# Making some of a layer's products one layer earlier: nine blocks' direct products in a four-layer sparse graph kernel

## The chip, the cores and the metric

The kernel runs on one core of a Trainium2 chip. The metric is the device time of one execution in microseconds (us). Three runs of the kernel before took 962.64, 964.93 and 965.73 us; the median is 964.93.

A core has five engines that work beside each other, each going through its own list of instructions in order: PE (TensorE, the matrix products), DVE (VectorE), ACT (ScalarE), POOL (GpSimd, which here starts the gathers) and SP (SyncE, which here starts plain transfers). Products are added up in PSUM, everything else lies in SBUF.

## The reference: what is computed

`x` has 2708 rows of 512 numbers; `adj` is a 2708 x 2708 matrix, nearly all zeros, whose nonzeros are denser towards low rows and low columns. Four layers follow, each `x = layernorm(x + gnn(x))`. The two that the change touches:

```python
# layer 0
adj_hat = adj + eye
d = 1 / sqrt(adj_hat.sum(axis=1))
gnn = (d[:, None] * adj_hat * d[None, :] @ x) @ W.T + b
# layer 1
head = (adj > 0) / sqrt(number of positive entries in the row)
inc = adj + head                                  # the "incidence"
gnn = (inc @ x) / inc.sum(axis=1)
```

Layer 2 sums rows under attention weights and under `adj` itself, and uses the projection `h = x @ W_sa`; layer 3 uses signs of a weight matrix. All is float32.

## The kernel before: tiles, stages and order

**Blocks.** The rows are cut into 22 blocks of 128 (the last, block 21, has 20). Four loops, one for each layer, go over the blocks in one order: `sequence` = 0, 1, 21, 2, 3, ... 20. The place of a block in it is its *turn* (block 1 has turn 1, block 2 turn 3, block 11 turn 12, block 12 turn 13, block 13 turn 14).

**Tiles.** For a block, only the columns of `adj` that hold a nonzero in its rows matter. A preparing stage (to about 199 us) finds them and packs the block's part of `adj` into tiles of 128 columns, `packed[b]`. There are two kinds:
- *direct* tiles: a whole block of columns taken as it lies (column block 0 or 1, the dense ones). `DIRECT` lists them: 20 tiles in 15 blocks. Their rows of `x` already lie in SBUF (`place_of_x(0)`, `place_of_x(1)`), so nothing is fetched.
- *gathered* tiles: 98 in all. The 128 rows of `x` that belong to the packed columns are fetched by an indirect DMA that POOL starts (`gathered`, the transfer at L626) into one of a ring of buffers `xg`. After every few gathers a memset (L636) pauses POOL. Some gathered tiles are *narrow*: they serve only 32 or 64 of the block's 128 rows; two to four of them, for different rows, run beside each other on PE.

Every product of a tile is issued by `add_tile` (L1393). One 128 x 512 float32 product shows as two PE instructions in the profile.

**Layer 0** (about 200 to 353 us). For each block: gathers from `y_rows` (ten buffers), the products, then on DVE the combination with the block's own rows (L1508) and the layernorm, which leaves the new x1 in SBUF, and a write of these rows to `x1_rows` in HBM. Two turns behind, `grow1` (L1445 to L1459) adds the finished block's share to block 0's sum of layer 1, `sum1`: block 0 is so dense that it takes every block of columns as it lies; DVE makes the incidence (L1450, L1453) and PE the product (L1454). Beside that, the table `between` hands small steps to the turns. Those that matter here are the head values of layer 1: the blocks lie in nine groups (`GROUPS`), and group n has its positive entries counted at turn 2 + 2n and the row of its values, `head_row`, kept at turn 3 + 2n (L1239). So the direct tiles of a block can be used for layer 1 only when x1 of blocks 0 and 1 is there, and the incidence only when its group's `head_row` is.

**Layer 1** (about 353 to 569 us). For each block but 0: gathers from `x1_rows` (eight buffers, a pause after every two), the incidence of all its tiles on DVE (two operations for each run of tiles, L1674 and L1675), the products (direct tiles first, then whole gathered ones, then narrow ones, `in_turns`), and `finish1`: ACT makes the own share, `t = own1 * x1` (L1586), DVE adds `rdeg` times the sum in PSUM (L1587), then layernorm and a write to `x2_rows`. Then `project1` makes `h` of an earlier block for layer 2 (four transposes L1612, sixteen products L1619), and `grow2` adds to block 0's sums of layer 2 (L1652, L1653).

**Layers 2 and 3** (to the end) take `x2_rows` and what follows in the same manner (gathers L1820, products L1844, L2099, L2138).

**What sets the order.** The program is traced in the order of its Python; a scheduler then fixes the order of instructions of every engine when the program is built. POOL's gathers are chained to one another and to the pauses in the order in which they are traced. On the chip, each engine follows its list, and waits at an instruction until what it needs is there.

Two lines tell where direct and gathered tiles part:

```python
nd = len(direct(b))
src = {i: place_of_x(direct(b)[i]) for i in range(nd)}
```

Of the kernel before, what the change touches and what calls it, by code (L numbers as in the profile page):

```python
# [8 lines left out]
F32 = mybir.dt.float32  # L9
# [10 lines left out]
P = 128  # L20
# [36 lines left out]
)  # L57


WHOLE3 = 5  # L60
AHEAD3 = 5
FETCHES3 = 3
# [445 lines left out]
def sparse_layers(ctx, tc, x, adj, adj_t, w0_t, b0, w_sa, a_sa, w_gcnb, b_gcnb, wa, ba, wb, bb, w3_t,  # L508
# [26 lines left out]
    def tiles(b: int) -> int:  # L535
        return len(direct(b)) + ROOM[b]
# [815 lines left out]
        t, spans = i - len(direct(b)), SPANS[SPLIT[b]]  # L1352
        return spans[t][1:] if 0 <= t < len(spans) else (0, rows(b))

    def whole_runs(b: int, most: int, apart: bool = False):

        nd, n = len(direct(b)), narrow(b)
        whole = [i for i in range(tiles(b)) if not nd <= i < nd + n]
        runs = []
        for i in whole:  # L1360
            if runs and sum(runs[-1]) == i and runs[-1][1] < most and not (apart and i == nd + n):
                runs[-1] = (runs[-1][0], runs[-1][1] + 1)
            else:
                runs.append((i, 1))
        return runs
# [31 lines left out]
    def last_of(b: int, i: int, order):  # L1397
# [3 lines left out]
            span(b, j)[1] <= r0 or span(b, j)[0] >= r1 for j in order[order.index(i) + 1 :]  # L1401
        )

    sum1 = ps_mm.tile([P, D], F32, tag="sum1", name="l1_0", bufs=1)
    with tc.tile_pool(name="s_l0", bufs=10, reuse_waits="tile") as lp:


# [37 lines left out]
        def grow1(j: int):  # L1445

            r = rows(j)
            inc = lp.tile([P, P], F32, tag="inc0", name=f"inc0_{j}", bufs=2)
            a = packed[0][:r, j, :]
            nc.vector.scalar_tensor_tensor(  # L1450
                inc[:r], a, 0.0, head0_row[0][:r], op0=ALU.is_gt, op1=ALU.mult
            )
            nc.vector.tensor_tensor(inc[:r], inc[:r], a, op=ALU.add)  # L1453
            nc.tensor.matmul(  # L1454
                sum1, inc[:r], place_of_x(j)[:r, :D], start=(not grown1),
                stop=(len(grown1) == NB - 1),
            )
            grown1.append(j)

        between = {  # L1460
            2: [attention_loads], 4: [lambda: attention_columns(0)],
# [21 lines left out]
        for at, b in enumerate(sequence):  # L1483
            m = rows(b)
            old = place_of_x(b)
            nc.vector.tensor_tensor(old[:m, :D], old[:m, :D], b0_row[:m], op=ALU.add)
            if b:
                nd = len(direct(b))
                order_ = in_turns(b)
                src = {}  # L1490
                for i in order_:
                    if i >= nd:
                        src[i] = gathered(lp, D, y_rows, b, i - nd)
                    else:
                        if direct(b)[i] == b:
                            y_direct[b] = lp.tile([P, D], F32, tag="own", name=f"y_own{b}", bufs=1)
                            nc.sync.dma_start(y_direct[b][:m], y_rows[b * P : b * P + m, :])
                        src[i] = y_direct[direct(b)[i]]
                ps = ps_mm.tile([P, D], F32, tag="mm", name=f"l0_{b}")
                for i in order_:  # L1500
                    r0, r1 = span(b, i)
                    add_tile(ps, b, i, packed[b][:, i, r0:r1], src[i][:, :D], order_)
            else:
                ps = sum0
            if at > 1:
                grow1(sequence[at - 2])
            t = work.tile([P, D], F32, tag="t", name=f"t0_{b}")
            nc.vector.scalar_tensor_tensor(  # L1508
                t[:m], ps[:m], dinv[:m, b : b + 1], old[:m, :D], op0=ALU.mult, op1=ALU.add
            )  # L1510
            layernorm(old[:m, :D], t, m, f"0_{b}")
            nc.sync.dma_start(x1_rows[b * P : b * P + m, :], old[:m, :D])
            for step_ in between.get(at, []):
                step_()
        for b in sequence[-2:]:
            grow1(b)
    l0_ps.close()
# [64 lines left out]
    def finish1(b: int, ps):  # L1582
        m = rows(b)
        new, old = pairs.get(b, (f[b], f[b]))
        t = work.tile([P, D], F32, tag="t", name=f"t1_{b}")
        nc.scalar.activation(t[:m], old[:m, :D], AF.Copy, scale=own1[:m, b : b + 1])  # L1586
        nc.vector.scalar_tensor_tensor(  # L1587
            t[:m], ps[:m], rdeg[:m, b : b + 1], t[:m], op0=ALU.mult, op1=ALU.add
        )
        layernorm(new[:m, :D], t, m, f"1_{b}", on_act=True)  # L1590
        nc.sync.dma_start(x2_rows[b * P : b * P + m, :D], new[:m])

    with tc.tile_pool(name="s_l1", bufs=8, reuse_waits="tile") as lp:
# [67 lines left out]
        for at, b in enumerate(sequence):  # L1661
            m = rows(b)
            if b:
                nd = len(direct(b))
                order_ = in_turns(b)
                src = {i: place_of_x(direct(b)[i]) for i in range(nd)}
                for i in order_:
                    if i >= nd:
                        src[i] = gathered(lp, D, x1_rows, b, i - nd)
                ps = ps_mm.tile([P, D], F32, tag="mm", name=f"l1_{b}")  # L1670
                inc_of = {}

                def incidence(iv, a, row):
                    nc.vector.scalar_tensor_tensor(iv, a, 0.0, row, op0=ALU.is_gt, op1=ALU.mult)  # L1674
                    nc.vector.tensor_tensor(iv, iv, a, op=ALU.add)  # L1675

                for i0, n in whole_runs(b, 3):
                    inc = lp.tile([P, 3, P], F32, tag="inc0", name=f"inc{b}_{i0}", bufs=3)
                    iv = inc[:, :n, :m]
                    incidence(  # L1680
                        iv, packed[b][:, i0 : i0 + n, :],
                        head_row[:, None, b * P : b * P + m].to_broadcast([P, n, m]),
                    )
                    for i in range(n):
                        inc_of[i0 + i] = iv[:, i, :]
                inc = lp.tile([P, P], F32, tag="inc1", name=f"incn{b}", bufs=3)
                for i0, r0, w, a in narrow_views(b):
                    n = a.shape[1]
                    at_ = b * P + r0
                    iv = inc[:, r0 : r0 + n * w].rearrange("p (n i) -> p n i", n=n)  # L1690
                    incidence(
                        iv, a,
                        head_row[:, at_ : at_ + n * w].rearrange("p (n i) -> p n i", n=n),
                    )
                    for i in range(n):
                        inc_of[i0 + i] = iv[:, i, :]
                for i in order_:
                    add_tile(ps, b, i, inc_of[i], src[i][:, :D], order_)
            else:
                ps = sum1  # L1700
            if left and left[0][-1] in sequence[: max(at - 2, 0)]:
                grow2(left.pop(0))
            finish1(b, ps)
            if at:
                project1(sequence[at - 1])
            if at == 1:
                open_block(0, wp2, ps_mm, "mm")
                open_sums(0)
# [521 lines left out]
```

## Time and profile before

One execution was profiled. It took 992.0 us in all; the profile spans 990.3 of it, with a mean granted PE clock of 0.946. That is 2.8% more than the median of the unprofiled runs (964.93).

| | busy, us | share of the span |
|---|---|---|
| PE, products | 860.8 | 87% |
| DVE | 654.7 | 66% |
| POOL | 549.4 | 55% |
| ACT | 381.1 | 38% |

| stage | us from the span's start |
|---|---|
| preparing, packing, projecting | 0 to 199 |
| layer 0 | 199 to 353 |
| passage: last x1 rows written, first gather of them issued at 359.12, its product at 363.58 | 353 to 364 |
| layer 1 | 364 to 569 |
| layers 2 and 3 | 569 to 990 |

How to read it: an engine's busy time is what its instructions took, not what they had to take; a share of 87% is a mean over stages, some of which leave PE no idle time and some of which do. What a moved instruction costs depends on what its engine does at the place from which it is taken and at the place to which it goes, and on who waits for it there.

### The profile page before, as it was taken

How to read it: one execution, taken by the hardware profiler on the slowest of the kernel's cores; microseconds unless marked ns; L12 is line 12 of the kernel's file. 1: busy time of each engine (PE TensorE's matmuls, PEld its weight loads, DVE VectorE, ACT ScalarE, POOL GpSimd, SP SyncE). 2: the span in 40 equal slices, each digit the busy share in tenths (PEclk: the TensorE clock that was granted, in tenths of full speed). 3: DMA queues.
4: the chain of work that ended last, by engine and by line, in shares of the span. 5: the costliest groups of instructions: out<-in, count | busy, mean ns of one | idle time of the engine just before them, and what ended most of it. 6: DMA issues, size and time to landing. Idle time of an engine off the chain costs nothing.

```text
span 990.3 us, 12880 instructions
## 1 busy us (share of the span) xinstructions
PE 860.8 (87%) x3659; PEld 452.2 (46%) x3659; DVE 654.7 (66%) x2538; ACT 381.1 (38%) x822; POOL 549.4 (55%) x660
## 2 busy tenths in 40 slices
PE   1898789759979979999999989988999999599992
PEld 0444344212222324555555634543555555378771
DVE  4888888726657766565654446675888776556685
ACT  2665556100000014554544433333444333254653
POOL 2577888687877647776542054553454320066661
PEclk9998998979989989999999998998999999889996
DMA  9999996466777646777653276786777541299985
GB/s 266 339 336 306 301 310 199 142 193 192 237 211 222 207 132 195 223 220 233 183 176 121 97 249 236 257 276 216 249 274 261 174 149 47 85 316 331 308 249 173
DMA packets 93557, 220.06 MB, mean 222 GB/s; under 512 B 13660, under 2 KB 28364, under 8 KB 93476
## 3 DMA queue, kind: packets, MB, share of 16 engines
q0 software_dynamic: 43008, 127.61, 43.5%
q1 hardware_dynamic: 38520, 76.78, 22.6%
q10 hardware_dynamic: 11948, 14.76, 4.7%
q8 instruction: 31, 0.51, 0.2%
q14 instruction: 50, 0.41, 0.1%
HBM read 178.21 MB, written 31.71 MB: 212 GB/s over the span
## 4 chain that ended last, share of the span: by engine, by line
PE 68%; DVE 14%; DMA 7%; issue 5%; ACT 2%; another core or an unknown queue 2%; POOL 1%; SPq 0%; ACTq 0%; DVEq 0%; POOLq 0%
PE l L1393 17%; PE h L1619 8%; PE e L1844 7%; PE a L1844 7%; PE l L2099 4%; PE pg L1892 4%; PE pc L1892 3%; PE y L1127 3%; PE l L2138 2%; PE l L1454 2%; PE e L1652 2%; PE a L1653 2%; PE px L1953 2%; DVE s_mask L895 2%; DMA xg<-x_rows,i 2%
## 5 line engine op out<-in xcount | busy, mean ns | idle before, releaser
L1093 POOL DMA_INDIRECT a<-in_adj_t_dram,row_at x98 | 111.3, 1136 | 58.7 <-DVE deg L838 26.1
L626 POOL DMA_INDIRECT xg<-x_rows,i x98 | 95.8, 978 | 70.7 <-PE l L1393 37.1
L626 POOL DMA_INDIRECT xg<-y_rows,i x98 | 97.7, 997 | 32.6 <-issue 19.0
L1393 PE MATMUL l<-xg,a 128*32 128x512 f32 (+3 forms) x196 | 86.0, 646 | 12.6 <-DMA xg<-y_rows,i 12.6
L1820 POOL DMA_INDIRECT xg<-x_rows,i x60 | 59.1, 986 | 61.8 <-ACT ae L1575 16.3
L1127 PE MATMUL y<-s_w,xt 128*128 128x512 f32 (+1 forms) x176 | 91.3, 667 | 1.7 <-ACT xt L1119 1.7
L626 POOL DMA_INDIRECT xg<-xw_rows,i x70 | 71.3, 1018 | 38.7 <-issue 15.9
L1820 POOL DMA_INDIRECT a<-x_rows,i x38 | 36.9, 970 | 95.1 <-DVE mask L1578 37.1
L1619 PE MATMUL h<-s_wsa,xt 128*128 128x256 f32 (+3 forms) x352 | 81.9, 385 | 0.0
L1619 PEld LDWEIGHTS h<-s_wsa,xt 128*128 128x128 f32 (+1 forms) x352 | 63.9, 186 | 24.8 <-ACT xt L1614 9.2
L830 ACT ACTIVATE unused<-arow 128x1408 uint8<-128x1408 f32 (+3 forms) x44 | 58.3, 1325 | 3.0 <-DMA x_rows<-s_zero 2.0
L663 ACT ACTIVATE rsqs<-mv 128x1 f32<-128x1 f32 (+2 forms) x56 | 11.3, 202 | 120.7 <-DVE mv L692 58.8
L1844 PE MATMUL a<-xg,a 128*32 128x512 f32 (+2 forms) x120 | 51.2, 629 | 4.3 <-DMA xg<-x_rows,i 4.3
L1127 PEld LDWEIGHTS y<-s_w,xt 128*128 128x128 f32 (+1 forms) x176 | 35.6, 213 | 41.9 <-issue 39.6
L2099 PE MATMUL l<-ws,pw 128*128 128x512 f32 (+1 forms) x210 | 50.8, 394 | 1.7 <-issue 1.2
L1844 PE MATMUL e<-xg,ae 128*32 128x512 f32 (+2 forms) x120 | 47.9, 601 | 1.1 <-issue 1.1
L694 POOL TENSOR_TENSOR rs<-mv,s_neg_half 128x1 f32<-128x1 f32 (+1 forms) x22 | 13.0, 592 | 61.4 <-DVE mv L692 52.0
L1892 PE MATMUL pg<-s_wg,pt 128*128 128x256 f32 (+1 forms) x176 | 45.0, 397 | 1.3 <-ACT pt L1880 1.3
L688 DVE BATCH_NORM_STATS2 st<-t 128x6 f32<-128x512 f32 (+1 forms) x66 | 45.3, 687 | 0.3
L916 PE MATMUL find<-s_sides,s_mask 128*128 128x5 bf16 (+1 forms) x462 | 15.7, 166 | 34.1 <-DVE s_mask L912 25.2
L2099 PEld LDWEIGHTS l<-ws,pw 128*128 128x128 f32 (+1 forms) x210 | 39.4, 190 | 11.9 <-issue 2.9
L1393 PEld LDWEIGHTS l<-xg,a 128*32 128x32 f32 (+3 forms) x196 | 19.8, 146 | 54.4 <-issue 38.6
(307 smaller groups left out, 1995.5 us busy)
## 6 DMA issues: line engine op xcount, KB each, us to landing
arow<-in_adj_dram SPq DMA_DIRECT2D x21, 704.0 KB
arow<-in_adj_dram SPq DMA_DIRECT2D x21, 650.0 KB
x_rows<-f SPq DMA_DIRECT2D x40, 256.0 KB
aw<-in_adj_t_dram SPq DMA_DIRECT2D x21, 320.0 KB
y_rows<-yt ACTq DMA_DIRECT2D x20, 256.0 KB
x_rows<-h SPq DMA_DIRECT2D x19, 257.0 KB
f<-in_x_dram SPq DMA_DIRECT2D x19, 256.0 KB
h_own<-x_rows SPq DMA_DIRECT2D x19, 256.0 KB
```

What stands on the lines that cost most here:

```text
L626: nc.gpsimd.indirect_dma_start(out=t, out_offset=None, in_=src[:, :], in_offset=bass.IndirectOffsetOnAxis(ap=index[b][:, i : i + 1], axis=0),)
L688: nc.vector.bn_stats(st[:m], t[:m])
L830: nc.scalar.activation(unused[:m, : ar.shape[1]], ar, AF.Copy, accum_out=row_sums[:m, b, h : h + 1])
L895: nc.vector.tensor_scalar(mask[:m, c0 : c0 + ar.shape[1]], ar, 0.0, None, op0=ALU.not_equal)
L1093: nc.gpsimd.indirect_dma_start(out=packed[b][:, t + len(direct(b)), :], out_offset=None, in_=adj_t, in_offset=bass.IndirectOffsetOnAxis(ap ...
L1127: nc.tensor.matmul(ps[:m], xt[:, k, :m], w0[:, k, :], start=(k == 0), stop=(k == KC - 1))
L1393: nc.tensor.matmul(ps[r0:r1], weights, moving, start=(i == order[0]), stop=last_of(b, i, order))
L1619: nc.tensor.matmul(ps, xt[:, k, :m], w[:, k, :], start=(k == 0), stop=(k == KC - 1))
L1820: nc.gpsimd.indirect_dma_start(out=g, out_offset=None, in_=x2_rows[:, :], in_offset=bass.IndirectOffsetOnAxis(ap=index[b][:, t : t + 1], a ...
L1844: nc.tensor.matmul(ps[r0:r1], weights, moving, start=(i == order[0]), stop=last_of(b, i, order))
L1892: nc.tensor.matmul(ps, pt[:, k, :m], w[:, k, :], start=(k == 0), stop=(k == KC - 1))
L2099: nc.tensor.matmul(whole[b], p[:r, h, b * P : (b + 1) * P], g[:r, :], start=(j == 0 and h == 0), stop=(j == NB - 1 and h == 1),)
```

## The change

Layer 1's direct products of nine blocks are made in layer 0. A new function `begin1(b)`, called at the end of a turn of layer 0's loop, makes for block b: the incidence of its direct tiles (two DVE operations), their products into a PSUM buffer of their own (two buffers in turn, `sum0` and `t`), the own share `f[b] = own1 * x1` on ACT, and `f[b] += rdeg * sum` on DVE. The turn is the later of the block's own turn plus two and 4 + 2n for its group n, and only turns up to `BEGUN_BY` = 14 are taken: turn 4: block 1; 6: blocks 2 and 3; 8: 4 and 5; 10: 7; 11: 8; 12: 9; 14: 11. These are twelve direct tiles (blocks 1, 3 and 5 have two). The other eight (blocks 13, 14, 15, 16, 17, 20) stay where they were.

In layer 1 those nine blocks then start with their first gathered tile; `finish1` leaves out the ACT copy for them, and its DVE operation takes `f[b]` in place of it. The number of gathers and their order on POOL stay as they were.

The diff, with the moved helper `incidence` (now in one place for both layers) cut out at its old place:

```diff
+BEGUN_BY = 14
...
-    def whole_runs(b: int, most: int, apart: bool = False):
+    def whole_runs(b: int, most: int, apart: bool = False, since: int = 0):
...
-        whole = [i for i in range(tiles(b)) if not nd <= i < nd + n]
+        whole = [i for i in range(since, tiles(b)) if not nd <= i < nd + n]
...
+    def incidence(iv, a, row):
+        nc.vector.scalar_tensor_tensor(iv, a, 0.0, row, op0=ALU.is_gt, op1=ALU.mult)
+        nc.vector.tensor_tensor(iv, iv, a, op=ALU.add)
+
     sum1 = ps_mm.tile([P, D], F32, tag="sum1", name="l1_0", bufs=1)
+    begun = set()
...
+        def begin1(b: int):
+
+            m, n = rows(b), len(direct(b))
+            inc = heads.tile([P, 2, P], F32, tag="incd", name=f"incd{b}", bufs=2)
+            iv = inc[:, :n, :m]
+            incidence(
+                iv, packed[b][:, :n, :],
+                head_row[:, None, b * P : b * P + m].to_broadcast([P, n, m]),
+            )
+            pool, tag = ((ps_mm, "sum0"), (ps_t, "t"))[len(begun) % 2]
+            ps = pool.tile([P, D], F32, tag=tag, name=f"l1d_{b}", bufs=1)
+            for i, j in enumerate(direct(b)):
+                nc.tensor.matmul(
+                    ps[:m], iv[:, i, :], place_of_x(j)[:, :D], start=(i == 0), stop=(i == n - 1)
+                )
+            nc.scalar.activation(
+                f[b][:m], place_of_x(b)[:m, :D], AF.Copy, scale=own1[:m, b : b + 1]
+            )
+            nc.vector.scalar_tensor_tensor(
+                f[b][:m], ps[:m], rdeg[:m, b : b + 1], f[b][:m], op0=ALU.mult, op1=ALU.add
+            )
+            begun.add(b)
+
+        to_begin = {}
+        for b in sorted(DIRECT):
+            at = max(sequence.index(b) + 2, 4 + 2 * GROUPS.index(group_of[b]))
+            if at <= BEGUN_BY:
+                to_begin.setdefault(at, []).append(b)
...
             for step_ in between.get(at, []):
                 step_()
+            for c in to_begin.pop(at, []):
+                begin1(c)
...
-        nc.scalar.activation(t[:m], old[:m, :D], AF.Copy, scale=own1[:m, b : b + 1])
+        own = f[b] if b in begun else t
+        if b not in begun:
+            nc.scalar.activation(t[:m], old[:m, :D], AF.Copy, scale=own1[:m, b : b + 1])
         nc.vector.scalar_tensor_tensor(
-            t[:m], ps[:m], rdeg[:m, b : b + 1], t[:m], op0=ALU.mult, op1=ALU.add
+            t[:m], ps[:m], rdeg[:m, b : b + 1], own[:m, :D], op0=ALU.mult, op1=ALU.add
         )
...
-                order_ = in_turns(b)
+                first = nd if b in begun else 0
+                order_ = [i for i in in_turns(b) if i >= first]
...
-                for i0, n in whole_runs(b, 3):
+                for i0, n in whole_runs(b, 3, since=first):
```

More of the change, by code (lines that the diff above doesn't have):

```diff
@@ L1671, in sparse_layers @@
                 inc_of = {}
-                def incidence(iv, a, row):
-                    nc.vector.scalar_tensor_tensor(iv, a, 0.0, row, op0=ALU.is_gt, op1=ALU.mult)
-                    nc.vector.tensor_tensor(iv, iv, a, op=ALU.add)
-                for i0, n in whole_runs(b, 3):
+                for i0, n in whole_runs(b, 3, since=first):
                     inc = lp.tile([P, 3, P], F32, tag="inc0", name=f"inc{b}_{i0}", bufs=3)
```

## The prediction, made before the changed kernel was run

> **What bounds the kernel now.** I read the page's totals first, then its chain of work.
>
> ```profile
> span 990.3 us, 12880 instructions
> PE 860.8 (87%) x3659; PEld 452.2 (46%) x3659; DVE 654.7 (66%) x2538; ACT 381.1 (38%) x822; POOL 549.4 (55%) x660
> PE 68%; DVE 14%; DMA 7%; issue 5%; ACT 2%; another core or an unknown queue 2%; POOL 1%; SPq 0%; ACTq 0%; DVEq 0%; POOLq 0%
> ```
>
> PE carries two thirds of the chain. The change moves PE work from layer 1 (about 353 to 569 us) into layer 0 (about 200 to 353 us), so I need the busy time of both, window by window. Columns: window, length, busy us of PE, PEld, DVE, ACT, POOL, then the granted PE clock.
>
> ```profile
> 222.00:257.00 35.00, 32.70 (x87) 8.97 (x85) 23.47 (x94) 1.59 (x7) 27.54 (x32) 0.93 0.70 204
> 257.00:284.00 27.00, 21.08 (x75) 6.04 (x74) 16.92 (x70) 1.28 (x6) 22.07 (x26) 0.96 0.77 226
> 284.00:331.00 47.00, 42.40 (x146) 12.52 (x144) 31.47 (x150) 3.85 (x14) 36.07 (x43) 0.95 0.76 224
> 331.00:353.00 22.00, 21.53 (x59) 6.98 (x59) 17.60 (x90) 2.08 (x9) 8.66 (x10) 0.92 0.49 154
> 353.00:364.00 11.00, 7.08 (x11) 2.50 (x11) 7.71 (x33) 3.36 (x6) 4.11 (x5) 0.69 0.34 101
> 400.00:464.00 64.00, 64.00 (x265) 36.47 (x264) 35.87 (x147) 34.20 (x58) 47.81 (x61) 1.00 0.74 221
> 464.00:559.00 95.00, 95.00 (x353) 54.44 (x353) 47.70 (x183) 43.93 (x75) 37.39 (x47) 1.00 0.49 150
> ```
>
> From 400 on PE has no idle time. Layer 0 from 222 to 353 leaves PE 13.3 us idle (2.3, 5.9, 4.6, 0.5), 5.1 of it after 284, where the last four moved tiles lie. PE's timeline tells what the idle is and what the tiles cost (start, us, engine, line, operation, idle before).
>
> ```profile
> 277.26 1.10 PE L1393 MATMUL l<-xg,a 128*128 128x512 f32 x2
> 282.79 2.07 PE L1454 MATMUL l<-f,inc 128*128 128x512 f32 x2 [4.43 <-DVE t L1508]
> ...
> 360.03 3.75 PE L1393 MATMUL l<-f_other,inc 128*128 128x512 f32 x4 [2.19 <-DVE mv L690]
> 363.58 1.96 PE L1393 MATMUL l<-xg,inc 128*128 128x512 f32 x4
> ...
> 397.21 1.26 PE L1393 MATMUL l<-xg,incn 128*32 128x512 f32 x8
> ```
>
> The largest hole, 4.43 us, is a block-0 product waiting for VectorE. At 360 block 1's two direct tiles run while its gathers are still in flight. A 128x512 tile is two instructions whose starts lie 0.43 apart: 0.86 us.
>
> Layer 1 also hangs on the gathers that POOL issues:
>
> ```profile
> 393.59 0.95 POOL L626 DMA_INDIRECT xg<-x_rows,i  x1 [0.16 <-issue]
> ...
> 409.33 0.95 POOL L626 DMA_INDIRECT xg<-x_rows,i  x1 [0.30 <-issue]
> ```
>
> The first is block 3's last gather, and its product starts at 397.68 (inside the row at 397.21), 4.1 us later: it ran as soon as it landed. The second is block 5's last. From 386 to 416 POOL runs without a pause of its own, one gather per 1.4 us; only later does it wait for PE to free buffers, as POOL's waits in 385 to 560 show (total, times, longest):
>
> ```profile
> POOL xg L626 <- PE l L1393: 37.1, 16, 6.8
> ```
>
> So layer 1 is held by gathers to about 416 and by PE after it.
>
> **What the Trainium skill says.** (1) "TensorE: Matmul & The Clock Gate", section "What's actually happening": after an idle window (about 3.4 us) PE drops to half clock and needs about as long a busy window to return. The trace agrees: after the 4.43 us hole the clock records show 0.5 from 281.8 to 288.6, and the products at 360.03 take 0.9 us an instruction against 0.43. (2) Same page, "Step-by-step: what each phase is for": matmuls start and complete in program order. So a product that waits for a gather holds all PE work behind it; the 4.43 us wait agrees. (3) "DMA: Bandwidth & Descriptors", "Anatomy of one DMA — SWDGE (gpsimd) path": some 2.0 us plus bytes by rate, which makes an estimate of 2.6 us for a gather of 256 KB. The trace has 4.1 to 4.8 us from issue to product (359.12 to 363.58 for the first of layer 1); the measurement decides.
>
> **The change part by part.** The sum is made against the profiled execution, 992.0 us (span 990.3), 2.8% above the median of 964.93; the result is scaled by 964.93/992.0 = 0.9727.
>
> Durations, by form:
>
> ```profile
> L1508 DVE SCALAR_TENSOR_TENSOR t<-l,s_dinv,f 128x512 f32<-128x512 f32 x19 | 14.3, 750 | 21.9 <-PE l L1393 14.3 <-issue 4.8 <-remote 2.2
> L1674 DVE SCALAR_TENSOR_TENSOR inc<-a,s_head_row 128x128 f32<-128x128 f32 x24 | 6.9, 286 | 15.1 <-PE l L1393 7.2 <-issue 5.0 <-PE xt1p L1612 2.8
> L1675 DVE TENSOR_TENSOR inc<-inc,a 128x128 f32<-128x128 f32 x24 | 6.9, 287 | 0.3
> L1586 ACT ACTIVATE t<-f,s_own 128x512 f32<-128x512 f32 x19 | 13.7, 720 | 0.5
> ```
>
> *Layer 0, PE.* Twelve tiles: block 1's two at turn 4, blocks 2 and 3 (three) at 6, blocks 4 and 5 (three) at 8, then one each at 10, 11, 12, 14. At 0.86 us, with about 0.05 more each where shapes change: 10.8 us. Separate groups of narrow tiles (which run together and cost about 1 us a group) go from 44 to 43 over both layers: taken as nothing, 1 us either way. What absorbs it: the order that the built program gives PE puts the three tiles of blocks 4 and 5 just ahead of the 4.43 us wait and moves that waiting product about a block later. Products there trail landed gathers by only 0.2 to 2 us (257 to 277), so PE's delay from the five earlier tiles is caught up against the gathers. I let all but 1.0 us of the 5.9 idle be filled: 4.9. With the hole the half clock after it shortens: half of 3.4 us, 1.7. From 284 on products trail landed gathers by 5 to 11 us, so PE sets the end there; of the other 7.4 us idle I let 2.7 be filled, since the waits for VectorE stay. Cost: 10.8 - 4.9 - 1.7 - 2.7 = +1.5 us. Bounds: -1.7 (all fits, and the clock is kept) and +10.8 (nothing fits, all lies on the path to the last row of x1).
>
> *Layer 0, VectorE and ScalarE.* Incidence: six single blocks at 0.57 and three double ones at 0.84 (128x256 takes 420 ns for each of the two), 6.0 us; nine combinations at 0.75, 6.75; together 12.7 us on an engine that is 63 to 67% busy from 222 to 331. ScalarE gets nine copies at 0.72, 6.5 us, on an almost idle engine. I cost them at nothing beyond PE's unfilled idle; if VectorE's gaps are not where they fall, up to 0.75 + 0.85 is added to one layernorm at a time, and the next block-0 product waits that much longer. The new wait: a begun product waits for its incidence; behind it on PE stand the next block's gathered products, and behind those only buffers, for which POOL does not wait before 331. POOL's order is unchanged; on SP only writes of layer 1's rows change places, and no such write is waited for in layer 1.
>
> *The passage.* Layer 1's first gather (359.12) waits for the last x1 row, its first product for that gather (363.58). Block 1's two tiles fill that wait today: removing them gains nothing.
>
> *Layer 1 up to block 6.* Eight tiles go (1, 2, 3, 4, 5). In the new order the projection of block 0 stands behind all of block 1's gathered products; today parts of it fill the waits between them. That costs about what block 2's tile saves, and block 3's end stays tied to the gather of 393.59: +0.35. Block 4 gains 1.3. But block 5's last gather lands near 413.8, and the new order places its products before a projection (3.5 us) that runs first today, so PE stalls about 2.5 us, and about 1.1 at block 6. Walked through, block 6 ends 0.4 later than now.
>
> *Layer 1 from block 7.* PE-bound: blocks 7, 8, 9, 11 lose a tile each, 4 x 0.86 = 3.4. Layer 1: 0.4 - 3.4 = -3.0. Bounds: 0, and -8.6 (ten tiles outside block 1). ScalarE's and VectorE's removed work (6.5 and 6.0 us) hides behind a full PE. Layers 2 and 3 keep their order.
>
> *Sum.* +1.5 - 3.0 = -1.5: 990.5, times 0.9727 = 963.5 us.
>
> **The rivals.** *A, faster.* Layer 0 hides everything, and gathers run ahead so that all ten tiles count: 992.0 - 8.6 = 983.4, or 956.6. For it: 13.3 us idle against 10.8, and PE full from 400 on. Against: the gather of 393.59 used on landing.
>
> *B, slower.* Layer 0 is bound by PE around the moved work: the holes are waits for VectorE, which is now busier, so they persist. A quarter (2.7) is absorbed: +8.1 - 3.0 = +5.1, 997.1, or 969.9. For it: products trailing by 5 to 11 us after 284. Against: the slack at 257 to 277. It decides once layer 0 costs over 6.0, that is absorbs under 4.8 of 10.8 (half-clock gain included).
>
> *C, nothing comes of it.* Gathers hold all of layer 1: +1.5, 993.5, or 966.4. Against: 37.1 us in which POOL waits for PE.
>
> **How the numbers follow.** About 0.3% (2.9 us) is what a measurement of this kernel can tell from no change. Forecast (layer 0 at 0 to 3, layer 1 at -2 to -5), 963.5, own range 960 to 966.5: chance 0.45, of which 0.13 faster, 0.30 same, 0.02 slower. A: 0.25, faster. B: 0.26, slower. C: 0.04, same. Sums: 0.38, 0.34, 0.28. The range takes in A's and B's values with about 1 us around them: 956 to 971; beyond lie the far ends of both bounds together (954.9 and 975.4).
>
> **What would show it.** Right: the last gather of layer 0 still issues near 343 and its last product ends 0 to 3 us later; the 4.43 us hole shrinks; block 3's last narrow product still starts about 4.1 us after its gather; a new stall at block 5; layer 1 is 2 to 5 us shorter. Wrong towards A: layer 1 shorter by over 6 us, with products trailing gathers all through blocks 3 to 6. Wrong towards B: layer 0 over 6 us longer, with new waits of PE for the begun incidence or for row sums.

## The result, and the profile after

The change makes the kernel slower. Over six runs of each, its median is 970.59 us (970.44 to 973.38) and that of the kernel before 963.76 us (958.73 to 965.73): a ratio of 1.0072 with a 95% interval of 1.0048 to 1.0095, or 7 us (4.6 to 9.2). A second comparison, made later (`after_2` below), gave 1.0073 (1.0048 to 1.0098). The prediction had said 963.5.

The page of the changed kernel begins as follows.

```profile
span 971.4 us, 12877 instructions
PE 861.2 (89%) x3641; PEld 453.8 (47%) x3659; DVE 664.6 (68%) x2547; ACT 382.4 (39%) x822; POOL 549.0 (57%) x660
PE 62%; DVE 12%; DMA 11%; POOL 7%; issue 5%; ACT 3%; ACTq 0%; SPq 0%; POOLq 0%; DVEq 0%
```

The profile spans 971.4 us (973.4 in all, the longest of the six runs, 0.3% above their median). The one shown for the kernel before spans 990.3 us (992.0 in all, 2.8% above its median), so the two traces can't be set against each other: by them the change would win 19 us. I therefore profiled the kernel before again (run `again` below: span 962.2 us, 963.9 in all). All comparisons from here on use that trace. The stages are cut where POOL issues the first gather of a layer, which can be read from the gathers' lines (durations in ns as minimum, median and maximum, then start of the first and of the last in us). `again`:

```profile
L626 POOL DMA_INDIRECT xg<-y_rows,i x98: 944/949/2247, 194.7 to 332.6; - x98
L626 POOL DMA_INDIRECT xg<-x_rows,i x98: 944/949/1418, 344.5 to 516.5; - x98
```

The changed kernel:

```profile
L627 POOL DMA_INDIRECT xg<-y_rows,i x98: 942/947/1351, 195.1 to 331.2; - x98
L627 POOL DMA_INDIRECT xg<-x_rows,i x98: 941/946/1413, 351.5 to 523.8; - x98
```

Layer 0, from its first gather to the first of layer 1, takes 344.5 - 194.7 = 149.8 us before and 351.5 - 195.1 = 156.4 after. The gathers themselves are no later (137.9 and 136.1 us from first to last). The loss is in the passage from the last gather of layer 0 to the first of layer 1: 11.9 us before, 20.3 after. PE is behind at the end of layer 0, and layer 1 can't begin before the last block is done. Layer 1, counted to the first gather of layer 2, takes 210.1 us before and 210.6 after: nothing is given back, although twelve products are gone from it.

A block's own figure is the time from the issue of its gather to the start of its product, worked out from the two timelines. For the first gather of blocks 12, 14, 16, 18 and the last gather of block 20 it is 4.4, 5.5, 7.7, 6.8 and 3.9 us in `again`, and 5.2, 8.3, 12.2, 12.4 and 10.6 in the changed kernel. Up to block 13 the first gathers show 3.6 to 6.4 us in `again` and, but for the 8.1 of block 9, 3.6 to 7.1 in the changed kernel: products follow landed gathers in both. From block 14 on PE falls behind in the changed kernel and stays behind, while `again` has caught up at the end.

### The profile page after: what moved, and what is told of

The parts are those of the page before. It is cut to its first block, busy times and chain, and to the rows that moved or that the text cites. A ratio compares the mean times of both kernels' runs of the same rounds, so it can differ in the third digit from the quotient of the medians.

```text
span 971.4 us, 12877 instructions
## 1 busy us (share of the span) xinstructions
PE 861.2 (89%) x3641; PEld 453.8 (47%) x3659; DVE 664.6 (68%) x2547; ACT 382.4 (39%) x822; POOL 549.0 (57%) x660
## 4 chain that ended last, share of the span: by engine, by line
PE 62%; DVE 12%; DMA 11%; POOL 7%; issue 5%; ACT 3%; ACTq 0%; SPq 0%; POOLq 0%; DVEq 0%
PE l L1394 11%; PE h L1658 7%; PE a L1880 7%; PE e L1880 6%; PE l L2135 5%; PE l L2174 4%; PE pg L1928 4%; PE pc L1928 3%; POOL xg L627 3%; PE y L1128 3%; DMA xg<-y_rows,i 3%; DMA xg<-x_rows,i 3%; DMA arow<-in_adj_dram 2%; POOL a L1094 2%; PE px L1989 2%
## 5 line engine op out<-in xcount | busy, mean ns | idle before, releaser
L1394 PE MATMUL l<-xg,a 128*32 128x512 f32 (+3 forms) x196 | 88.9, 623 | 6.9 <-DMA xg<-y_rows,i 6.3
L1128 PEld LDWEIGHTS y<-s_w,xt 128*128 128x128 f32 (+1 forms) x176 | 36.2, 217 | 40.9 <-issue 40.8
L896 DVE TENSOR_SCALAR s_mask<-arow 128x1408 bf16<-128x1408 f32 (+3 forms) x42 | 40.3, 959 | 5.3 <-DMA arow<-in_adj_dram 5.3
```

Of the source, the lines that this page charges most:

```text
L896: nc.vector.tensor_scalar(mask[:m, c0 : c0 + ar.shape[1]], ar, 0.0, None, op0=ALU.not_equal)
L1128: nc.tensor.matmul(ps[:m], xt[:, k, :m], w0[:, k, :], start=(k == 0), stop=(k == KC - 1))
L1394: nc.tensor.matmul(ps[r0:r1], weights, moving, start=(i == order[0]), stop=last_of(b, i, order))
```

## The experiments

Each ratio is against runs of the kernel before on the same chip. Layer 0, the passage that is its last part, and layer 1 are from one profile each; kernels with the same order and work in layer 0 differ there by up to 2.6 us (`tail` and `tail_l1`), and `pe_only`, whose layer 1 has the work of before, takes 2.6 more there than `again`. So a stage's difference under 3 us says little by itself.

| run | ratio (95% interval) | layer 0 | its passage | layer 1 |
|---|---|---|---|---|
| again | 1.0003 (0.9988 to 1.0018) | 149.8 | 11.9 | 210.1 |
| the change; after_2 | 1.0072 (1.0048 to 1.0095); 1.0073 (1.0048 to 1.0098) | 156.4; 155.8 | 20.3; 18.9 | 210.6; 208.1 |
| cost_alone | 1.0110 (1.0082 to 1.0137) | 156.2 | 18.9 | 210.1 |
| gain_alone | 0.9993 (0.9977 to 1.0010) | 149.9 | 11.8 | 208.3 |
| by8 | 1.0090 (1.0058 to 1.0122) | 155.4 | 17.6 | 211.5 |
| split | 1.0068 (1.0043 to 1.0094) | 154.9 | 17.6 | 210.3 |
| order_only | 1.0059 (1.0036 to 1.0082) | 153.2 | 15.2 | 210.4 |
| pe_only | 1.0061 (1.0042 to 1.0080) | 154.1 | 16.3 | 212.7 |
| tail | 1.0089 (1.0065 to 1.0112) | 154.8 | 16.6 | 208.9 |
| pinned | 1.0049 (1.0034 to 1.0063) | 155.8 | 15.8 | 208.5 |
| pinned_pe_2 | 1.0048 (1.0028 to 1.0068) | 152.8 | 12.8 | 211.8 |
| tail_l1 | 1.0038 (1.0024 to 1.0053) | 157.4 | 16.7 | 204.5 |
| before_l1 | 1.0014 (0.9997 to 1.0032) | 151.3 | 12.1 | 210.4 |
| best | 0.9997 (0.9978 to 1.0016) | 155.5 | 15.8 | 203.6 |
| best_no1_2 | 0.9995 (0.9974 to 1.0016) | 155.4 | 15.8 | 202.6 |

Three more ran on a chip on which the kernel before takes 991.6 us, and are told at the end.

### The kernel before again, and the two halves of the change

The theories: **L0**, the loss lies in layer 0, on PE; **L1**, layer 1's new order loses what its missing products would bring. `again` is the kernel before, unedited.

> The kernel before, unchanged, for a second profile of it (the first ran 2.8% above the median). Both theories: ratio 1.000 within 0.003; a span near 962 us. From its trace: the time from the first gather of layer 0 to the first gather of layer 1 is to stand below the 159.5 us of the first profile. If layer 0 is where the change lost (theory L0), it stands at about 148 to 150, some 7 us below the 156.4 of the changed kernel, and layer 1 (first gather to layer 2's first) is not over 0 to 3 us longer than the changed kernel's 210.6. If layer 1 gave nothing or lost by its new order (theory L1), layer 0 differs by only 0 to 3 us and layer 1 takes 206 to 208.

`cost_alone` is the change with one line added at the end of layer 0, so that layer 1 works as before (its own share of the begun blocks is then taken from the begun sums):

```diff
         for b in sequence[-2:]:
             grow1(b)
+        begun.clear()
```

> The nine begun blocks are made in layer 0 as in the change, and layer 1 makes all its direct products again as before (the begun results are thrown away): the cost in layer 0 alone, with layer 1's order of before. Base 963.8. Theory L0 (PE bound in layer 0, the moved work mostly on the path): +8 to +10, 972 to 974. Theory L1 (layer 0 absorbs it, layer 1's new order loses): +1 to +3, 965 to 967.

`gain_alone` is the change with `begin1` emptied, so that nobody makes the twelve products (the own share stays in `finish1`):

```diff
         def begin1(b: int):
-            m, n = rows(b), len(direct(b))
...
             begun.add(b)
```

> Layer 1 leaves out the direct products of the nine blocks and nobody makes them (layer 1's sums lack these shares); layer 0 is as before. The gain in layer 1 alone, with layer 1's order of the change. Base 963.8. Theory L0: -2 to -4, 960 to 962. Theory L1: 0 to +5, 964 to 969, that is no gain or a loss although twelve tiles are gone. If the gathers ran ahead all through: -8.6, 955.

`by8` has `BEGUN_BY = 8` in place of 14.

> Only turns up to 8 are begun: blocks 1, 2, 3, 4, 5 (eight tiles), all ahead of the stretch of layer 0 in which products trail the gathers by 5 us and more. Theory L0 with the cost after 284 us: the early eight cost 0 to 3 and gain nothing in layer 1 (gathers hold it there), so 963 to 967, clearly below the 970.6 of the change. Theory L0 with the cost all along: 8 of 12 tiles, +5 to +7, 969 to 971. Theory L1 (order of the first blocks of layer 1): as slow as the change or slower, 970 to 973, since the late four tiles' gain is gone too.

Layer 0 alone costs 1.1%, 10.6 us (7.9 to 13.2) in all and 6.4 by the stage; layer 1 alone gives 0.7 us (-1.0 to 2.2, so not clear of nothing), 1.8 by the stage. The loss is in layer 0 (L0). But `by8` goes against my version of L0: without the four late tiles the cost hardly falls (8.7 us, 5.6 by the stage). Nothing is begun after turn 8 there, and still its products fall behind at the end. For the first gather of blocks 14, 16, 18 and the last of block 20 the time from issue to product is 6.1, 8.9, 8.1 and 8.5 us against 5.5, 7.7, 6.8 and 3.9. So something other than the late products slows PE at the end.

### The order of the narrow tiles

PE's timeline shows it. Block 17's two narrow tiles (64 rows each) in `again` (start, us, engine, line, operation, count):

```profile
322.86 0.49 PE L1231 MATMUL hr<-s_ident,hd 128*128 128x128 f32 x3
323.28 1.08 PE L1393 MATMUL l<-xg,a 128*64 128x512 f32 x4
324.29 1.12 PE L1454 MATMUL l<-f,inc 128*128 128x512 f32 x2
```

The same two tiles in the changed kernel:

```profile
326.57 1.07 PE L1394 MATMUL l<-xg,a 128*64 128x512 f32 x2
327.57 0.18 PE L1188 MATMUL hr<-s_sides,pos 128*128 128x1 bf16 x1
327.61 0.21 PE L1188 MATMUL hr<-valid,pos 128*128 128x1 bf16 x3
327.75 1.07 PE L1394 MATMUL l<-xg,a 128*64 128x512 f32 x2
```

Together the two tiles take 1.08 us; torn apart by a few tiny products, each takes 1.07. Of tiles that run together the Trainium skill says the same in "TensorE: Matmul & The Clock Gate", section "Measured speedup vs the span model": a pack of tiles takes about the time of one product. The scheduler, given nine more steps in layer 0, put PE's instructions in another order there. In blocks 14 and 16 to 20, where PE sets the end, each block's narrow tiles stand in two groups and not in one; in the early blocks, where gathers set the pace, there are fewer groups. The number over the layer is about the same (43 before, 42 after), and the place is worse. `by8` has blocks 14 to 20 all in two groups. That is theory **S**; **B** is that the moved work itself is the cost.

`tail` adds to the change a chain on PE from turn 15 on: each product is bound behind the one traced before it, with no wait added, so that the scheduler keeps the order of the Python (a block's tiles, then the block-0 product).

```diff
             if at > 1:
                 grow1(sequence[at - 2])
+            if at >= 15:
+                pe_chain(traced_, last_pe)
```

> The change, with one thing added: from layer 0's turn 15 on (blocks 14 to 20, turns in which nothing is begun) PE is bound to take a block's tiles and then the block-0 product in the order in which they are traced, as it did before the change. Four pairs of narrow tiles (blocks 16, 17, 18, 20) that the change's order had torn apart run together again, and one block-0 product fewer stands behind the last block. Theory S (the loss in layer 0 is the torn narrow tiles at its end, where PE sets the pace): 4 to 5 us of the change's 6.6 in layer 0 come back, 965 to 967 on a base of 963.4. Theory B (the moved products themselves lie on PE's path): 0 to 1 us come back, 969 to 971.

`split` is the kernel before with that chain, and with the block-0 product put between a block's narrow tiles:

```diff
                 for i in order_:
                     r0, r1 = span(b, i)
                     add_tile(ps, b, i, packed[b][:, i, r0:r1], src[i][:, :D], order_)
+                    if at >= 15 and i == nd:
+                        grow1(sequence[at - 2])
```

> The kernel before, with nothing moved: in layer 0's turns from 15 on, the block-0 product is put between a block's first narrow tile and the others, so that seven pairs of narrow tiles are torn apart. PE does the same products. Theory S: each tear costs 0.5 to 1.0 us where PE sets the pace, +4 to +7, 967 to 970, and the stretch from the last gather of layer 0 to the first of layer 1 grows from 11.9 to 16 to 18 us. Theory B: the order costs nothing by itself, 963 to 964.

`order_only` is the kernel before with PE's 280 instructions of layer 0 chained in the change's order (the change's 292 without the twelve new ones), and `pe_only` chains all 292 but takes the packed tiles as weights and leaves out VectorE's and ScalarE's part of `begin1`:

```diff
         for b in sequence[-2:]:
             grow1(b)
+        pin(ORDER0)
```

> The kernel before, nothing moved, no work added; only the order of PE's instructions in layer 0 is set to the one that the built program of the change has (its twelve products left out). So PE, VectorE and POOL do exactly the work of before, in the change's order. Layer 0, from its first gather to the first of layer 1, took 149.8 us before and 156.4 with the change. Theory S (the order, by its torn narrow tiles and late block-0 products, is the loss): 154 to 157 us there, +4 to +7 in all, 967 to 970. Theory B (the moved work is the loss): 150 to 151 there, 963 to 964 in all. In between: both.

> PE's side of the moved work alone: PE has exactly the change's order in layer 0, the twelve products with it, but they take the packed tiles as they are (no incidence made) and their sums are dropped (no copy on ScalarE, no combination on VectorE); layer 1 makes all its direct products as before. Against 'cost_alone' (156.2 us in layer 0, +10 in all), which has VectorE's and ScalarE's share too. If VectorE's 12.7 us and ScalarE's copies in its queue carry the loss: 150 to 152 in layer 0, 964 to 967. If PE's order and products carry it: 154 to 157, 968 to 974.

`split` costs 6.6 us with no work added (5.1 in layer 0, for seven tears: 0.7 each). `order_only` costs 5.7 us (3.5 to 7.9), 3.4 by the stage, with nothing set but PE's order. So the order alone makes half or more of the loss (5.7 of 6.9 in all, 3.4 of 6.6 by the stage). `pe_only` stands 0.9 above `order_only` in layer 0, within what the stages can tell, and level with it in all (1.0061 and 1.0059). `cost_alone`, which adds VectorE's and ScalarE's part to that, stands at 1.0110: about 4.7 us more in all, 2.1 by the stage.

`tail` missed: four pairs run together again, and only 1.6 us come back in layer 0, none in the total. Its chain had made a stall of its own. It put the counting of the last groups and block 11's begun product ahead of block 15, and these wait for VectorE:

```profile
312.22 0.20 PE L1204 MATMUL hr<-s_sides,pos 128*128 128x1 bf16 x2 [0.37 <-DVE rsqs L699]
...
313.55 0.18 PE L1204 MATMUL hr<-s_sides,pos 128*128 128x1 bf16 x1 [1.05 <-DVE pos L1202]
...
313.75 1.12 PE L1494 MATMUL l1d<-f_other,incd 128*128 128x512 f32 x2
...
315.98 1.13 PE L1476 MATMUL l<-f,inc 128*128 128x512 f32 x2 [0.95 <-DVE inc L1475]
316.94 1.02 PE L1410 MATMUL l<-f,a 128*128 128x512 f32 x2
```

From issue to product, block 15's first gather takes 14.4 us there, against 10.1 in the change; then, the pairs together, PE gains it back, to 8.4 at the last gather (10.6 in the change). The run doesn't decide between S and B.

### The moved work in the order of before

`pinned` is the change with PE chained in the order of before, the twelve products between blocks; `pinned_pe` has the products without VectorE's and ScalarE's part. A piece of the chain (t: tiles, g: block-0 products, B: begun products, H: counting):

```text
g2 t3_4 t4_0 t3_5 H2_17 H2_18 g3 t4_5 t4_6 t4_1 t4_2 t5_0 t4_3 t5_1 t4_4 g4 B0 B1 t5_6 t5_2 ...
```

> The change with all its moved work, but PE's instructions in layer 0 set to the order that the kernel before has, with the twelve products put between blocks of it (none tears narrow tiles; the last stands after block 14). Theory S: layer 0 loses only 1 to 2 us, 151 to 152, and with layer 1 as in the change 963 to 966 in all. Theory B: layer 0 at 155 to 158, 969 to 972.

> PE's side of the moved work alone, as in 'pe_only', but in the order of 'pinned' (the order of before, none of the narrow tiles torn): twelve products more on PE in layer 0, no more work for VectorE and ScalarE; the products take the packed tiles as they are and their sums are dropped; layer 1 makes all its direct products as before. 'pinned', with all the moved work, took 155.8 us from the first gather of layer 0 to the first of layer 1, the kernel before 149.8. If PE's time is the cost in this order: 153.5 to 156, +4 to +6 in all, 967 to 970. If VectorE's and ScalarE's work is: 150 to 152, 963 to 966.

`pinned_pe` fell on a chip on which the kernel before takes 991.6 us (told below), and was run again:

> 'pinned_pe' once more, since its chip ran the kernel before at 991.6 us where three others ran it at 963 to 964. On one of these: if PE's time is the cost of the moved work in the order of before, 153.5 to 156 us in layer 0 and +4 to +6 in all; if VectorE's and ScalarE's work is, 150 to 152 and 0 to +2. On a chip at 990, where PE has further waits in layer 0: 0 to +2 in all, as measured.

S alone falls here: with no pair torn the layer still takes 155.8 us, 6.0 more than before (all in all 4.7 us, 3.3 to 6.1). The products alone come to 152.8 (+3.0), so by the stages half of it goes with VectorE's and ScalarE's part; the totals (1.0048 and 1.0049) don't separate the two, since `pinned` has layer 1's gain as well. Where PE now waits in `pinned`, from 205 to 355 us (total, times, longest):

```profile
PE l L1508 <- DVE f L751: 2.7, 2, 1.6
PE hr L1234 <- DVE pos L1232: 2.5, 2, 1.9
PE l L1508 <- DVE mv L739: 1.6, 2, 1.2
PE l L1442 <- DMA xg<-y_rows,i: 1.2, 2, 1.0
```

The waits for gathers, 5.1 us in `again` over the same stretch, are down to 1.2; waits for VectorE are up from 4.6 (2.2, 1.6 and 0.8, shown further below) to 6.8.

Three parts of layer 0 show where each run loses: from its first gather to block 14's first product of gathered rows, from there to the end of block 20's last one, and from there to layer 1's first gather (us; in brackets PE's idle time).

| run | to block 14 | blocks 14 to 20 | to layer 1 |
|---|---|---|---|
| again | 109.7 | 33.3 (0.9) | 6.8 |
| before_l1 (below; same chain as `split`, one block torn) | 112.0 | 32.2 (0.4) | 7.1 |
| split | 110.1 | 37.9 (0) | 6.8 |
| order_only | 110.0 | 36.2 (1.1) | 7.0 |
| pe_only | 111.2 | 35.9 (0) | 7.0 |
| cost_alone | 110.4 | 37.1 (1.0) | 8.6 |
| the change | 110.8 | 37.1 (1.0) | 8.6 |
| pinned_pe_2 | 114.8 | 31.1 (0) | 6.9 |
| pinned | 117.6 | 31.3 (0) | 6.9 |

In the change's order most of the loss lies in blocks 14 to 20, where PE hardly waits and its own instructions take longer. Another 1.8 us comes behind them in the change and in `cost_alone`, but not in `pe_only`: VectorE works there without a wait (343.0 to 347.7 us in the changed kernel). In the order of before the loss lies ahead of block 14.

When PE's order is fixed, the scheduler changes VectorE's too. Of 425 instructions of VectorE in layer 0 that the runs share, all stand in one sequence in `again` and `gain_alone`, 361 in `again` and `split`, but only 250 in `again` and `order_only`, 275 and 282 with `pinned` and `pinned_pe_2`. In blocks 14 to 20 that can be no more than the 1.1 us for which PE waits in `order_only`; what part it has in the losses of the two pinned runs ahead of block 14 was not tried.

### Layer 1 in one order

`tail_l1` is `tail` with a chain in layer 1 too: a block's tiles, then the sixteen products of the projection of the block before it (chained in the same way). `before_l1` is the kernel before with the same two chains, and `best` is `pinned` with layer 1's chain.

```diff
                 for i in order_:
                     add_tile(ps, b, i, inc_of[i], src[i][:, :D], order_)
+                if at >= 3:
+                    pe_chain(traced_, last_pe)
```

> As 'tail', and in layer 1 PE takes the blocks from 2 on in one pattern: a block's gathered tiles, the narrow ones together, then the projection of the block before it. In the change's order the products of block 5's gathers stand ahead of a projection and wait for gathers, and block 12's narrow tiles are torn. Theory S for both layers: layer 1 (first gather to layer 2's first) shortens by 2 to 4 us against the 210.6 of the change, to 961 to 964 in all, level with or below the kernel before. Theory B, or gathers that hold layer 1 in any order: no further gain on 'tail'.

> The kernel before with the same two orders bound as in 'tail_l1' and nothing moved: what the orders alone do. Its layer 0 end is already in that order. Theory S: within 2 us of the kernel before, 961 to 965, so that any lead of 'tail_l1' over it is what moving the products is worth in a fair order (0 to 4 us). Theory B: as before, and 'tail_l1' 4 us or more above it.

> As 'pinned', and layer 1 in the one pattern of 'tail_l1' (which took 204.5 us there against 210.6 for the change and 210.4 for the kernel before in the same pattern). Theory S: 151 to 152 in layer 0 and 204 to 205 in layer 1, 958 to 960 in all, faster than the kernel before by 0.3 to 0.5%. Theory B: 965 to 968.

The gathers of `best`:

```profile
L648 POOL DMA_INDIRECT xg<-y_rows,i x98: 942/948/1540, 193.4 to 333.1; - x98
L648 POOL DMA_INDIRECT xg<-x_rows,i x98: 940/946/1195, 348.9 to 518.3; - x98
```

Layer 2's first follows at 552.5. Layer 1 falls from 210.6 to 204.5 and 203.6 us, 6 to 7 below the change and below `before_l1` (210.4), to which the same chain brings nothing. So the missing products are worth 6 to 7 us there, if no torn pair and no early stall eats them. `best` comes out even with the kernel before, not faster as was expected: +5.7 in layer 0, -6.5 in layer 1. `tail_l1` (967.0 in all) misses what was expected for the same reason: its layer 0 takes 157.4.

### Fewer tiles, and another chip

`best_no1` leaves block 1 out of the begun blocks, `best_2to5` begins blocks 2 to 5 only.

```diff
-            if at <= BEGUN_BY:
+            if b > 1 and at <= BEGUN_BY:
```

> As 'best', but block 1's two direct products stay in layer 1, where PE has nothing else to do while the first gathers are under way. If what layer 0 pays is PE's time beyond its waits for gathers, two products fewer save about 1.7 us there (155.5 to 153.8), and layer 1 (203.6) loses nothing: 961 to 962 in all, a ratio of 0.997 to 0.999. If layer 1 needs the room at its start: 204 to 206 there, and no gain.

> As 'best_no1', with blocks 2 to 5 alone begun (six tiles, about 5.2 us of PE), about what PE spends waiting for gathers in layer 0 (5.1 us). If what layer 0 pays is PE's time beyond those waits: 150 to 152 in layer 0; layer 1 loses 3.4 us (four tiles) against 'best', 206 to 208: 961 to 963 in all. If the layer-0 cost comes from the early tiles: 154 to 155 in layer 0 and 964 to 967 in all.

These two and `pinned_pe` ran on a chip on which the kernel before takes 991.6 us, near the 992.0 of the profile that the prediction used. There `pinned_pe` stands at 1.0007 (0.9984 to 1.0030), `best_no1` at 0.9950 (0.9925 to 0.9975) and `best_2to5` at 0.9995 (0.9970 to 1.0019); layer 0 takes 161.2, 166.5 and 161.3 us in their profiles, layer 1 210.1, 205.7 and 207.6 (159.5 and 210.1 in the profile that the prediction used). I took `pinned_pe`, `best_no1` and the change to one more chip:

> 'best_no1' once more, for the same reason. On a chip at 963: 153 to 155 us in layer 0, 204 to 206 in layer 1, a ratio of 0.996 to 1.000. On a chip at 990: 0.993 to 0.998, as measured.

> The change itself beside them on the same chip. On a chip at 963: 1.005 to 1.010, as measured. On a chip at 990, whose layer 0 leaves PE more idle time: if this idle time takes up part of the moved work, 0.998 to 1.003, which would also say that the prediction's sum was right for the execution it was made on and wrong for the others.

On that chip, where the kernel before takes 964.0, the same products cost 0.48% (`pinned_pe_2`) that cost nothing on the other, and `best_no1_2` is even with the kernel before. Leaving out block 1 doesn't shorten layer 0 (155.4 against 155.5): what layer 0 pays isn't in proportion to the tiles. `best_no1` is the only version that was faster than the kernel before, by 0.5% on the one chip, and it is level with it on the other, where the change is 0.7% slower. The change was not run on the chip at 991.6 us.

## Why the prediction was wrong

**The profile it stood on.** "I let all but 1.0 us of the 5.9 idle be filled: 4.9", with 1.7 for the half clock after it, is the term that failed first. That idle time, its 4.43 us hole above all, isn't there in an execution at the median. PE's largest waits in layer 0 of the profile that the prediction used (219 to 359 us):

```profile
PE l L1454 <- DVE t L1508: 4.4, 1, 4.4
PE l L1393 <- issue: 3.7, 1, 3.7
PE hr L1187 <- issue: 3.5, 4, 1.2
PE l L1454 <- DVE rsqs L682: 2.3, 1, 2.3
```

and in `again` (205 to 355 us):

```profile
PE l L1393 <- DMA xg<-y_rows,i: 5.1, 10, 1.1
PE l L1393 <- DVE mv L690: 2.2, 1, 2.2
PE l L1454 <- DVE f L704: 1.6, 1, 1.6
PE hr L1187 <- DVE pos L1185: 0.8, 1, 0.8
```

The large holes are gone; what is left to fill are ten short waits for gathers, 5.1 us, and 3.8 us in the passage that nothing moved can fill. The 1.7 had nothing to save either: the mean granted PE clock from 205 to 341 us is 1.00 in `again`. (The clock record that the prediction quotes has the half clock last for 5.8 us after the hole, not for 3.4.) And that from 284 on "products trail landed gathers by 5 to 11 us" is less true at the median: for the first gathers of blocks 11, 12, 14 and 16, issue to product takes 11.6, 10.0, 12.2 and 12.4 us in the profile that the prediction used, and 5.0, 4.4, 5.5 and 7.7 in `again`. Of the 10.8 us of products, I let 9.3 be absorbed; by the stages 4.4 were (layer 0 +6.4, bounds given -1.7 to +10.8). I had noted the 2.8% and answered it by scaling the sum, which scales the holes and doesn't remove them.

The holes were not the chance of one execution either. The three profiles taken on the chip at 991.6 us have them too: PE's longest wait in their layer 0 is 3.2 (`pinned_pe`), 5.8 (`best_no1`) and 5.8 us (`best_2to5`), and no more than 2.2 in any profile from the other chips, the wait for the layer's first gathers aside. In all four of these long profiles VectorE waits there, 1.0 to 4.7 us at a time, for something that the profile's page puts down to "another core or an unknown queue" and its views call `remote`; in the other sixteen it never does in layer 0. In the profile that the prediction used (VectorE's waits, 205 to 359 us), and in `best_2to5` (VectorE's and PE's, 205 to 363 us):

```profile
DVE t L1508 <- remote: 4.7, 2, 2.5
...
DVE t L1610 <- remote: 4.7, 1, 4.7
...
PE l L1458 <- DVE t L1610: 5.8, 1, 5.8
```

So, as far as these profiles show, idle time of the kind that I read goes with executions of some 990 us and is absent from those of some 963 to 973, among which the result was measured. On which chip the first profile was taken is not on record, and what `remote` stands for stays open.

**The order.** "Separate groups of narrow tiles ... go from 44 to 43 over both layers: taken as nothing" failed. The figures are off (the traces have 43 and 42 groups in layer 0 alone, 23 and 22 more in layer 1), but that the number hardly changes is right; the groups became fewer in the early blocks and more where PE sets the end, and the order alone costs 3.4 us in layer 0. A sum over the layer hid that.

**VectorE and ScalarE in layer 0.** "I cost them at nothing beyond PE's unfilled idle" failed: by the stages they make some 3.0 of 6.0 us in the order of before, and in the change's order `cost_alone` stands 4.7 us above `pe_only` in all. The durations were right: nine combinations took 6.7 us against 6.75. A wait that I didn't see is among the causes that may be behind it: ScalarE's copy overwrites x1 of its block and so waits for the block-0 product that reads it, in the changed kernel

```profile
ACT f L1481 <- PE l L1460: 13.9, 5, 4.9
```

with the row of head values and the next layernorm's step behind it in ScalarE's queue (at 308.95 the copy, at 309.58 and 309.93 these two). What share it has was not tried.

**Layer 1.** -3.0 was said; `gain_alone` has -1.8 by the stage and the change -2.0 and +0.5. The end of the walk came true, in part by luck: counted from the layer's first gather, block 6's last narrow product comes 0.5 us later in `gain_alone` than before (66.05 and 65.58), near the "block 6 ends 0.4 later than now". But block 3's comes 0.7 earlier, where the walk has +0.35, block 4's 2.3 and block 5's 4.1 (54.6 and 58.7), and block 6's narrow tiles are torn, which the walk didn't have. Block 11 then leads by 1.7, not 3.0: block 9's narrow tiles are torn too, and its lead falls from block 8's 1.3 to 1.0 though a tile is gone there. (In the change's order block 12's are torn.) POOL's own pauses, a memset of 0.43 us after every two gathers, are inside the 1.4 us a gather from 386 to 416, which the prediction read as unpaused. In the changed kernel's profile PE also waits 2.19 us for a gather of block 1, and by block 2's last narrow product it is 1.9 us behind `after_2` (31.9 and 30.0 us), which is most of what separates the two stages:

```profile
361.39 1.98 PE L1394 MATMUL l<-xg,incn 128*32 128x512 f32 x4 [0.45 <-DVE inc L1406]
365.56 2.58 PE L1394 MATMUL l<-xg,incn 128*32 128x512 f32 x4 [2.19 <-DMA xg<-x_rows,i]
```

**The rivals.** The prediction's B gave 969.9 and 970.59 came; that it comes so near is in part luck. Its mechanism holds in part: layer 0 costs over 6.0, PE is behind at its end, and waits for VectorE persist. But it had +8.1 in layer 0, where +6.4 was measured, and it didn't have the torn pairs. Nor did its sign come, "new waits of PE for the begun incidence": no begun product in the changed kernel has idle time of PE before it. What is new are waits for the incidence of the block-0 product, of which `again` has none (205 to 355 us):

```profile
PE l L1460 <- DVE inc L1459: 3.3, 3, 1.4
```

A's claim that all ten tiles count in layer 1 is near what `best` shows there, in an order that the change doesn't have.

**What stays open.** In the change's own order the parts measured one by one are 3.4 (order), 0.9 (products) and 2.1 (the rest: 156.2 - 154.1); in the order of before 3.0 and 3.0. They don't add up across the orders: what falls behind in one place can fill waits in another, and VectorE's order is different in each run. The total of `cost_alone` (10.6 us, its interval reaching down to 7.9) exceeds its stage (6.4). In the profiles most of the rest lies in layer 2 (first gather to layer 3's first), 294.0 us there and 291.1 in `again`; but that stage takes anything from 290.0 to 295.8 us in the profiles from the chips at 963 to 964, so whether the change has a hand in it isn't settled.

## What to carry to other kernels

Moved work is worth what its old place pays and costs what its new place lacks: read both from an execution that runs at the median, or take another profile, because an execution well above it can show holes that the others don't have, and scaling the sum doesn't take them out. When a scheduler sets the order, a step added in one place reorders the engine far from it; compare the two orders by place, not by count, and where PE sets the end look whether tiles that ran together still do. If the move is worth keeping, chain the order by hand first: here that made the missing products worth 6 to 7 us in layer 1, as much as the move costs in layer 0.

## What the runs showed of the hardware that I had not expected

The same program took 963 to 964 us on four chips and 991.6 on a fifth. The difference is in more than one stage: on the fifth, layer 3 took 123.1 to 126.5 us in the three profiles taken there, and 116.2 to 118.2 in all those taken on the others; in layer 0 its profiles have the waits for `remote` shown above. The same products (`pinned_pe`) that cost 0.48% on one of the four show no cost on the fifth (1.0007, 0.9984 to 1.0030).
